# The second half of an attention layer cut into pairs, its routing moved with it, and the experts' weights loaded into tiles that an earlier layer has left

## The chip, the cores and the metric

The kernel runs on one core of one Trainium2 chip, as one program with one launch. The metric is the device time of that program in microseconds (us), the median of several executions. One further execution, the profiled one, left the trace from which all durations below come.

## The reference: what is computed

The input is x, 8 sequences of 128 tokens with 128 features, a context of 8 x 77 tokens with 128 features, and a mask. Eight blocks follow each other, each added to x: an attention over the context (L0_xattn, 16 heads of 8), a soft mixture over slots with a two-matrix feed-forward (L0_ffn), a second attention over the context (L1_xattn, 16 heads of 64), a routed mixture of 64 experts (L1_ffn), and then four larger blocks (L2_xattn, six local-attention layers, L3_xattn, two local-attention layers). All arithmetic is float32. The change touches the second attention and the routed experts. Cut to what matters, these compute:

```python
# L1_xattn, for each sequence b, 16 heads of 64
q = layernorm(x) @ w_q; k, v = split(context @ w_kv)
x = x + tanh(gate) * (softmax(q * 64**-0.5 @ k.T) @ v) @ w_out + b_out ...
# L1_ffn, over all 1024 tokens
logits = layernorm(x) @ gate_w + gate_b            # 64 experts
top3 values and experts; gates = softmax over the three
place of a token in its expert = number of earlier tokens that chose it; kept if place < 64
y[e] = gelu(rows[e] @ w1[e] + b1[e]) @ w2[e] + b2[e]   # 64 rows for each of 64 experts
x = x + sum over the kept choices of gate * y
```

The place of a token needs the choices of all tokens before it, and an expert's rows need the choices of all tokens, so the experts can start only when the last sequence has been routed.

## The kernel before, in words

**How the order is made.** The kernel is not written in execution order. Functions add steps to a plan (`Plan.add`): which engine, an estimated cost, what is read and written, which tiles are opened. `Plan.arranged` then walks through a model of time and gives each free engine the ready step of the lowest rank (the order in which steps were added), if there is room for the tiles it opens. The result is a fixed order of instructions on each engine, written into the program. TensorE (PE) gets small filler matmuls (L733) wherever this model leaves it without work in the first part, to keep its clock up. Each engine, and the queue of the sync engine SP that issues the transfers, runs its own list strictly in order.

**Tiles.** Working tiles come from pools by size: 49 tiles called `big` (512 columns), 3 `huge` (1232 columns), small ones, and 8 PSUM banks `mm`. Two large tiles, `wide` (3072 columns) and `narrow`, hold the weights of L0 (`wide`) and the padded values of its attention (`narrow`), and later the keys and values of L2_xattn. They hold nothing between the end of L0 and the fourth eighth of the experts.

**L1_xattn** (`plan_xattn_64`) works on halves of four sequences: normalize, transpose, then for each group of 8 heads the keys of all four (one matmul of 4 x 77 columns for each 128 features), the queries of all four (512 columns), and then sequence by sequence scores, softmax, values, output projection. `finish` (L1081) adds a sequence's result to x. A sequence is done after its second group.

**Routing** (`Routed.some`) takes a run of sequences: normalize (DVE statistics, POOL for the inverse root, L798 to L815, and ACT or DVE for the scaling), transpose, logits (L1310, L1311), the three best on DVE (L1320, L1322), their places (L1340 to L1358), row numbers (L1368 to L1372), and then three indirect transfers for each sequence, issued by POOL (L1387), that put the normalized rows into `expert_rows` in DRAM. It is called for sequences 0 to 3, for 4 and 5, for 6, and for 7. In the plan 4 and 5 come when the second group of sequence 5 is added.

**Experts** (`Routed.experts`, `Routed.four`): eight reads (L1445) bring `expert_rows` back, transposes turn them into `slots`. Then for each pair of experts two matmuls up (L1485), a copy, four transposes, a bias (L1495), a gelu (L1498), and eight matmuls down (L1506). Every expert needs two weight transfers of 256 KB (L1469), 128 in all, each into a `big` tile. They stand on SP's queue: 37 of them before the eight reads, 91 behind. `SPARE = 12` is the number of `big` tiles that such a prefetch must leave free in the plan; `EARLY = 4` experts are asked for at the start.

**Gates** (`Routed.gates`): the gates' normalization (L1406 to L1409), a spread of them over the experts (L1418, L1420), two more small matmul steps (transposes and L1429) and an addition to x (L1432). The plan adds them in the middle of the experts, but lets them be taken up to 600 steps ahead.

Of the kernel before, what the change touches and what calls it, by code (L numbers as in the profile page):

```python
# [24 lines left out]
P = 128  # L25
# [511 lines left out]
class Plan:  # L537
# [14 lines left out]
    def __init__(self, tc, rooms):  # L552
        self.tc, self.rooms, self.steps, self.also = tc, {k: list(range(n)) for k, n in rooms.items()}, [], []
        self.left = {k: int(self.LEFT * n + 0.9) for k, n in rooms.items()}
        self.last = {k: n // 3 for k, n in self.left.items()}
        self.latest, self.previous = {}, None
        self.warm, self.until = None, 0.0

    def fixed(self, tile):
# [48 lines left out]
    def arranged(self):  # L608
        rooms, free = self.rooms, dict.fromkeys(self.TAIL, 0.0)
# [13 lines left out]
        first = 0  # L623
        left, extra, done_on_pe = sum("PE" in s.ns for s in self.steps), 0, True

        def open_to(s):
            need = Counter(v.tag for v in s.opens)
            ahead = s.rank - first
            leaves = {k: 0 if ahead < self.NEXT // 2 else self.last[k] if ahead < self.NEAR else n for k, n in self.left.items()}
            return all(len(rooms[k]) >= n + (s.spare if s.spare and ahead else leaves[k]) for k, n in need.items())  # L630

        while times:
            t = heapq.heappop(times)
            while back and back[0][0] <= t:
                _, _, tag, slot = heapq.heappop(back)
                rooms[tag].append(slot)
            while coming and coming[0][0] <= t:
                s = heapq.heappop(coming)[2]
                for e in s.ns:
                    heapq.heappush(came[e], (s.rank, s))  # L640
            for e in free:
                if free[e] > t:
                    continue
                kept, pick, held = [], None, set()
                while came[e]:
                    rank, s = heapq.heappop(came[e])
# [10 lines left out]
                if pick is None:  # L657
                    if e == "PE" and t < self.until and t >= free[e] + (self.IDLE if done_on_pe else 0.0) and (
                            rooms["mm"] and left and (coming or any(free[x] > t for x in free if x != e))):
                        s = Step(first, {e: self.WARM}, self.warm(rooms["mm"][-1]), None, None, 0, None)  # L660
# [14 lines left out]
                s = pick  # L675
# [320 lines left out]


BUFS_A = {"tiny": 30, "few": 3, "row": 6, "big": 49, "huge": 3, "w": 1, "wr": 1}
EARLY = 4
SPARE = 12  # L1000


def plan_front(w, early, dram, wide, narrow):

    c, nc, plan, a = w.c, w.c.nc, w.plan, w.c.a
    c.room("w1", early)

    places = Context.places(plan, wide, narrow)
    lo, vals = 0, {}
    for name in ("wa", "wb", "w0"):  # L1010
        n = a[name].shape[1]
        c.packs[name], vals[name] = wide[:, lo : lo + n], plan.part(places[0], lambda t: t)
        lo += n
    come = {}

    def load(name, ns, emit, vals=None):
        come[name] = plan.fixed(None)
        plan.add({"SP": ns}, emit, [], [come[name], *(vals or [])])

    def pack(name, ns):  # L1020
        load(name, ns, lambda e: c.load(name))


    masks = [w.tile([P, 4, KC] if w.general else [KC, 4, P], I32) for _ in range(2)]
    sent = [0, 0]

    def soon(kb, emit, writes):
        sent[0] += 470
        sent[1] += kb
        plan.add({"SP": 470}, emit, [], writes, tail=max(2000.0, 2000.0 + 3.3 * sent[1] - sent[0]))  # L1030

    def x_in(b0, n):
        soon(64 * n, lambda e: nc.sync.dma_start(c.x[:, b0 : b0 + n, :], a["x"][b0 : b0 + n].rearrange("b s d -> s b d")),
              w.xs[b0 : b0 + n])

    def context(h):
        come["ctxT", h] = plan.fixed(None)
        at = slice(4 * h * KC, 4 * (h + 1) * KC)
        soon(154, lambda e: nc.sync.dma_start(c.ctxT[:, at], a["ctxT"][:, at]), [come["ctxT", h]])

    def mask(h):
        at = slice(4 * h, 4 * h + 4)
        soon(154, lambda e: nc.sync.dma_start(
            masks[h](), a["mask"][at].rearrange("b s k -> s b k") if w.general else a["maskT"][:, at, :]), [masks[h]])

    x_in(0, 2)
    soon(131, lambda e: c.load("wa"), [vals["wa"]])
    context(0)
    if w.general:
        mask(0)  # L1050
    soon(256, lambda e: c.load("wb"), [vals["wb"]])
    x_in(2, 2)
    context(1)
    x_in(4, 4)
    if w.general:
        mask(1)
    pack("col", 600)
    plan.add({"SP": 2500}, lambda e: c.load("w0"), [], [vals["w0"]])
    pack("row", 3800)
    pack("w1", 6500)  # L1060
    pack("cst", 3000)
    pack("wg", 200)
    if not w.general:
        mask(0)
        mask(1)
    route = Routed(w, early, dram, come)
    pack("w", 3000)
    pack("w3kv", 1700)
    for e in range(EARLY):
        route.weights(e)  # L1070

    tg = w.once.tile([P, 1], F32, name="tg")
    tgv = plan.fixed(tg)

    def gate(e):
        nc.scalar.activation(tg, c.get("row", "L1_xattn_gate"), AF.Tanh)
        nc.scalar.preload_act_table_set("natural_log_exp_and_others")

    def finish(b, out):
        x = w.xs[b]  # L1080
        plan.add({"DVE": 282}, lambda e: nc.vector.scalar_tensor_tensor(x(), out(), tg, x(), ALU.mult, ALU.add),  # L1081
                 [x, out, tgv], [x])

    l0x, vzs = plan_l0_xattn(w, masks, places[1], come, vals["wa"], vals["wb"])
    parts = ((0, 2), (2, 2), (4, 4))
    for part in parts:
        l0x(*part)
        plan.also = []
    plan.add({"ACT": 3000}, gate, [come["row"]], [tgv])
    if not w.general:  # L1090
        plan.add({"DVE": 2500}, lambda e: small_scores(c, (("L2_ffn", 6), ("L3_ffn", 2))), [come["row"]], [])
        for h in range(2):
            zero = w.tile([KC, 4, P])
            plan.add({"DVE": 600}, lambda e, h=h, zero=zero: nc.vector.tensor_scalar(
                zero(), masks[h](), 0.0, 2.0 * SUM_MOST, ALU.is_equal, ALU.mult), [masks[h]], [zero])
            plan.add({"DVE": 683}, lambda e, h=h, zero=zero: nc.vector.tensor_reduce(
                c.masked[:KC, h : h + 1], zero().rearrange("k b s -> k (b s)"), AX.X, ALU.max), [zero], [])
    plan.also = [vals["w0"], come["col"]]
    l0f = plan_l0_ffn(w)
    for part in parts:  # L1100
        l0f(*part)
    plan.also = [come["w1"], come["row"], come["col"]]
    l1x = plan_xattn_64(w, 8, c.get("w1", "L1_q"), c.get("w1", "L1_kv"),
                        c.get("w1", "L1_o").rearrange("p (c d) -> p c d", d=P), c.get("col", "L1_xattn_ln_gamma"),
                        c.get("col", "L1_xattn_ln_beta"), c.get("row", "L1_xattn_b_out"), finish)
    for _ in l1x(0):
        pass

    then = {3: (0, 4), 7: (4, 2), 8: (6, 1), 9: (7, 1)}
    for i, _ in enumerate(chain(l1x(1), [None]), 1):  # L1110
        if i in then:
            plan.also, also = [come["cst"], come["row"], come["wg"]], plan.also
            route.some(*then[i])
            plan.also = also
    plan.also = [come["col"]]
    route.experts(Context(w, places, vals.values(), vzs))
    plan.also = []
    return route

# [151 lines left out]
class Routed:  # L1271
# [24 lines left out]
    def some(self, b0, n):  # L1296

        w = self.w
        c, nc, plan = w.c, w.c.nc, w.plan
        at, xs = slice(b0, b0 + n), w.xs[b0 : b0 + n]  # L1300
        xh = w.tile([P, n, P])
        w.normed(lambda k: xh()[:, k, :], lambda k: xs[k](), xs, [xh], n=n)
        xT = w.tile([P, n, P])
        tp = w.turn(lambda k: xh()[:, k, :], [xh], opens=[xT], n=n)
        w.copy(xT, tp, [tp], [xT], 591, 682)
        lp, lg = w.bank([P, n, NE]), w.tile([P, n, NE])

        def logits(e):
# [7 lines left out]
        topv, efv, gatev = plan.fixed(top), plan.fixed(ef), plan.fixed(gate)  # L1316
# [14 lines left out]
        hot, chosen, before = w.tile([P, TOPK, n, NE]), self.chosen[:, at], self.before[:, at]  # L1331
# [22 lines left out]
        t, pos = w.tile([P, TOPK, n, NE]), self.pos[:, at]  # L1354
# [7 lines left out]
        validv, srcv, dstv = plan.fixed(valid), plan.fixed(srci), plan.fixed(dsti)  # L1362
# [35 lines left out]
    def gates(self, b0, n, hot, gatev, validv):  # L1398
# [9 lines left out]
            nc.vector.tensor_tensor(gate, gate, spread(gs, TOPK, 2), ALU.mult)  # L1408
            nc.vector.tensor_tensor(gate, gate, valid, ALU.mult)  # L1409

        plan.add({"DVE": 683}, weigh, [gatev, validv], [gatev])

        by_e, t2, by_eT = w.tile([P, n, NE]), w.tile([P, n, NE]), w.tile([NE, n, P])

# [4 lines left out]
                if k:  # L1419
                    nc.vector.tensor_tensor(by_e(), by_e(), t2(), ALU.add)  # L1420

        plan.add({"DVE": 5 * (200 + 75 * n)}, spread_gates, [hot, gatev], [by_e, t2])
        tp = w.turn(lambda k: by_e()[:, k, :], [by_e], NE, opens=[by_eT], n=n)
        w.copy(by_eT, tp, [tp], [by_eT], 591, 682)
        out = w.bank([P, n, P])
# [38 lines left out]
    def weights(self, e):  # L1464

        if e not in self.fetched:
            self.fetched[e] = pair = [self.w.tile([P, 4, P]) for _ in range(2)]
            for i, wt in enumerate(pair):
                self.w.plan.add({"SP": 870}, lambda _, wt=wt, i=i: self.w.c.nc.sync.dma_start(  # L1469
                    wt().rearrange("p c n -> p (c n)"), self.w.c.a["experts"][e, i]), [], [wt], spare=SPARE)  # L1470
        return self.fetched[e]

    def four(self, q, u, part, b1):

# [203 lines left out]
def plan_xattn_64(w, nch, wq, wkv, wo, gamma, beta, bias, finish, kept=None):  # L1678
# [61 lines left out]
            if j < n - 1:  # L1740
                yield

    return (part, ahead, kept) if kept else half 


class Kept:
# [660 lines left out]
```

## Time and profile before

| | |
|---|---|
| time of the runs | 1454.45 us median of 3 (1451.59 to 1457.88) |
| the profiled execution | 1436.21 us |
| its span (first to last instruction) | 1434.4 us |
| mean granted TensorE clock | 0.985 |
| busy, of the span | PE 93%, DVE 77%, ACT 59%, POOL 59% |
| last addition to x by L1_xattn | 250.48 us after the start of the span |
| first experts' matmul (L1485) | 280.40 us |
| last experts' matmul (L1506) | 373.2 us |
| first layer of local attention (L1919) | from 446.6 us |

All times inside the execution count from the start of the span. A "busy" PE includes the filler matmuls, so its share alone does not say how much of the time is needed. A float32 matmul leaves two records in the trace, a transpose one. "Idle before, releaser" is the time an engine stood still ahead of a group and what ended that; in a wait for the SP queue the releaser is what freed the tile or delivered the data.

### The profile page before, as it was taken

To read this page: it belongs to the slowest core of one execution; us is meant where nothing else is said; L and a number is where in the kernel's file an instruction comes from. 1 tells how busy PE (TensorE), PEld (TensorE's weight loads), DVE (VectorE), ACT (ScalarE), POOL (GpSimd) and SP (SyncE) were. 2 spreads that over 40 slices of the span, in tenths; PEclk is the share of its full clock that TensorE was granted. 3 is DMA by queue.
4 is the path that set the end of the run, shared out by engine and by line. 5 is a ranking of instruction groups with operands and counts; after the bars stand their busy time and mean duration, and the time that the engine had idled before them with its cause. 6 is when DMAs were issued, how large, how long until landed. Compare 5 with 4: busy or idle time off the path is not lost. (4 is left out here: it accounts for less than half of the span.)

```text
span 1434.4 us, 39795 instructions
## 1 busy us (share of the span) xinstructions
PE 1338.0 (93%) x15481; PEld 950.8 (66%) x15481; DVE 1109.2 (77%) x2350; ACT 850.7 (59%) x1775; POOL 842.3 (59%) x1367
## 2 busy tenths in 40 slices
PE   9999999898989899999999999999999999999996
PEld 7777767665576557567666676666666667665664
DVE  7543676433368898998999999999899996888882
ACT  5666565253435457567656676656667667666663
POOL 5210136401467887787687777777777772658661
PEclk9999999999989899999999999999999999999998
DMA  9401001389340357456445644754454553224330
GB/s 319 166 1 45 2 2 48 119 281 370 115 141 2 118 184 238 138 171 201 153 140 177 217 136 135 251 167 152 157 191 144 169 172 104 88 69 156 125 115 21
DMA packets 218781, 204.42 MB, mean 143 GB/s; under 512 B 31790, under 2 KB 167534, under 8 KB 217432
## 3 DMA queue, kind: packets, MB, share of 16 engines
q1 hardware_dynamic: 212696, 196.54, 42.0%
q0 software_dynamic: 1536, 3.15, 0.7%
q8 instruction: 124, 2.03, 0.6%
q10 hardware_dynamic: 4352, 2.10, 0.5%
q14 instruction: 73, 0.60, 0.1%
HBM read 129.49 MB, written 70.68 MB: 140 GB/s over the span
## 5 line engine op out<-in xcount | busy, mean ns | idle before, releaser
L1946 POOL TENSOR_TENSOR big<-big,big 128x512 f32<-128x512 f32 x224 | 284.6, 1278 | 110.8 <-DVE big L1943 87.8
L1919 PE MATMUL mm<-wide,big 128*128 128x512 f32 x672 | 310.8, 601 | 2.3 <-DVE y_res L2007 1.2
L771 ACT COPY big<-mm 128x512 f32<-128x512 f32 (+6 forms) x298 | 150.9, 517 | 157.0 <-PE mm L784 45.9
L1959 POOL TENSOR_TENSOR big<-big,few 128x512 f32<-128x512 f32 x224 | 227.4, 1043 | 1.9
L1798 DVE STREAM_TRANSPOSE big<-big 128x512 f32<-128x512 f32 (+1 forms) x248 | 209.9, 867 | 15.0 <-POOL big L1959 12.0
L1940 ACT ACTIVATE big<-mm 128x512 f32<-128x512 f32 x224 | 132.3, 596 | 144.9 <-PE mm L1919 139.8
L1919 PEld LDWEIGHTS mm<-wide,big 128*128 128x128 f32 x672 | 120.9, 191 | 124.3 <-issue 107.3
L1941 DVE TENSOR_TENSOR big<-mm,big 128x512 f32<-128x512 f32 x224 | 153.8, 687 | 13.8 <-ACT big L1940 11.5
L1943 DVE TENSOR_TENSOR big<-mm,big 128x512 f32<-128x512 f32 x224 | 153.3, 684 | 0.8 <-ACT big L1940 0.7
L1945 DVE TENSOR_REDUCE few<-big 128x8 f32<-128x512 f32 x224 | 151.5, 676 | 0.7 <-ACT big L1940 0.7
L2035 ACT ACTIVATE big<-mm 128x512 f32<-128x512 f32 x224 | 120.6, 600 | 35.0 <-PE mm L2028 32.3
L2003 PEld LDWEIGHTS mm<-narrow,big 128*128 128x128 f32 x896 | 108.9, 194 | 41.8 <-DVE big L2057 20.9
L2003 PE MATMUL mm<-narrow,big 128*128 128x128 f32 x896 | 116.8, 282 | 18.8 <-DVE big L2057 11.1
L2028 PEld LDWEIGHTS mm<-big,big 64*64 64x64 f32 x3584 | 124.9, 207 | 2.6 <-issue 1.9
L2028 PE MATMUL mm<-big,big 64*64 64x64 f32 (+2 forms) x3584 | 125.4, 274 | 1.2 <-DMA big<-blocks 1.1
L2095 PEld LDWEIGHTS mm<-big,big 128*32 128x32 f32 x3072 | 87.0, 110 | 28.9 <-issue 27.4
L2095 PE MATMUL mm<-big,big 128*32 128x128 f32 x3072 | 94.1, 273 | 0.5 <-issue 0.5
L784 PE MATMUL mm<-ident,big 128*128 128x128 f32 (+1 forms) x486 | 71.6, 282 | 24.2 <-DVE big L773 5.2
L784 PEld LDWEIGHTS mm<-ident,big 128*128 128x128 f32 (+1 forms) x486 | 54.7, 144 | 48.2 <-DVE big L773 10.5
L773 DVE COPY big<-mm 77x512 f32<-77x512 f32 (+5 forms) x89 | 52.5, 603 | 31.2 <-PE mm L1253 12.0
L2057 DVE SCALAR_TENSOR_TENSOR big<-mm,big 128x512 f32<-128x512 f32 x112 | 73.5, 684 | 1.9
L1495 DVE TENSOR_TENSOR big<-mm,p_col 128x512 f32<-128x512 f32 x32 | 20.7, 686 | 67.5 <-PE mm L784 57.5
(288 smaller groups left out, 2523.9 us busy)
## 6 DMA issues: line engine op xcount, KB each, us to landing
blocks<-big SPq DMA_DIRECT2D x224, 256.0 KB, 2.1
big<-blocks SPq DMA_DIRECT2D x224, 256.0 KB, 3.3
big<-in_experts_dram SPq DMA_DIRECT2D x128, 256.0 KB, 4.8
wide<-in_l2a_dram SPq DMA_DIRECT2D x6, 1536.0 KB, 8.9
narrow<-in_l2b_dram SPq DMA_DIRECT2D x6, 534.0 KB, 5.9
narrow<-in_l2o_dram SPq DMA_DIRECT2D x6, 512.0 KB, 6.3
blocks<-big SPq DMA_DIRECT2D x24, 128.0 KB, 1.7
big<-blocks SPq DMA_DIRECT2D x24, 128.0 KB, 3.1
```

What stands on the lines that cost most here:

```text
L771: nc.scalar.copy(out(), in_())
L1798: plan.add({"DVE": 150 + 138 * n}, lambda e: nc.vector.transpose(*within(u(), t())), [t], [u])
L1919: self.plan.add({"PE": 892}, lambda e: nc.tensor.matmul(ps(), lhsT=hs()[:, j, :], rhs=wqkv()[:, o : o + 512], start=True, stop=True), [hs, ...
L1940: yield lambda e: nc.scalar.activation(sq(), heads(), AF.Square)
L1941: yield lambda e: nc.vector.tensor_tensor(t1(), heads(), spread(rot()[:, 2 * kind, :], 8, 1), ALU.mult)
L1943: yield lambda e: nc.vector.tensor_tensor(halves(t2()), halves(heads())[:, :, ::-1, :], sin(), ALU.mult)
L1945: yield lambda e: nc.vector.tensor_reduce(ss()[:, lo : lo + 8], sq(), AX.X, ALU.add)
L1946: yield lambda e: nc.gpsimd.tensor_tensor(t1(), t1(), t2(), ALU.add)
L1959: plan.add({"POOL": 1062}, lambda e, t=t, t1=t1, i=i: nc.gpsimd.tensor_tensor(t().rearrange("p (c g d) -> p g c d", c=4, g=8), t1().rearra ...
L2003: nc.tensor.matmul(out(), lhsT=oT()[:, k, :], rhs=wo()[:, 4 * g + k, :], start=(g == 0 and k == 0), stop=(4 * g + k == nch - 1))
L2028: nc.tensor.matmul(sc[s]()[at : at + 64, k, q:end], lhsT=kT()[lo : lo + 64, k, at : at + 64], rhs=of_q(k, lo, q, end), start=False, stop=( ...
L2095: nc.tensor.matmul(avs[half]()[32 * t : 32 * t + 32, k, :], lhsT=vs[t // 2]()[:, at : at + 32], rhs=prs[t]()[:, k, :], start=True, stop=True)
```

## The change

Five edits in the first part of the program; everything from L2_xattn on stays as it is.

1. The second half of L1_xattn is normalized and transposed for its four sequences at once as before, but then runs in pairs: both groups of heads for sequences 4 and 5, then both for 6 and 7. Its keys come in matmuls of 2 x 77 columns and its queries in matmuls of 256 columns. The calls of the routing stay at steps 3, 7, 8 and 9 of it, so that sequences 4 and 5 are complete earlier than before. Routing of one or two sequences scales on DVE, and POOL's part of the normalization is two instructions instead of four.
2. The weights of experts 2 to 4 are loaded into `wide`, of 5 and 6 into `narrow`, of 7 into one `huge` tile (`weights_in`), once L0 has left them. Only experts 0 and 1 are asked for at the start.
3. The rule for the other prefetches asks for 14 free `big` tiles up to a point near the end of L1_xattn (`plan.calm`) and for 6 behind it. The plan's cost of one such transfer is 740 instead of 870.
4. The first two steps of the gates may be taken only 40 steps ahead of the oldest open step (`within=LATE`).
5. The keys and values of L2_xattn must wait for the experts whose weights lie in `wide` and `narrow`.

```diff
+            spare = s.spare and s.spare[self.calm is not None and first >= self.calm]
+            return all(len(rooms[k]) >= n + (spare if spare and ahead else leaves[k]) for k, n in need.items())
...
-EARLY = 4
-SPARE = 12
+SPARE, SPARE_LATER = 14, 6
+LATE = 40
...
-    for e in range(EARLY):
-        route.weights(e)
+    route.weights(0)
+    route.weights(1)
...
+    def idle(wide_was, narrow_was):
+
+        own = {0: [*wide_was], 1: [*narrow_was]}
+        for e, (k, lo) in enumerate(((0, 0), (0, 1024), (0, 2048), (1, 0), (1, 1024)), 2):
+            own[k] += route.weights_in(e, (places[k], lambda t, lo=lo: t[:, lo : lo + 1024]), own[k][: len((wide_was, narrow_was)[k])])
+        for e in range(7, 8):
+            route.weights_in(e, (w.tile([P, 1232]), lambda t: t))
+        return own[0], own[1]
...
+    plan.also = []
+    was = idle(vals.values(), vzs)
...
-    for _ in l1x(0):
+    for _ in l1x(0, 4):
...
-    for i, _ in enumerate(chain(l1x(1), [None]), 1):
+    for i, _ in enumerate(chain(l1x(4, 4, (0, 2), (2, 2)), [None]), 1):
+        if i == 8:
+            plan.calm = len(plan.steps)
...
-    route.experts(Context(w, places, vals.values(), vzs))
+    route.experts(Context(w, places, *was))
...
-        w.normed(lambda k: xh()[:, k, :], lambda k: xs[k](), xs, [xh], n=n)
+        w.normed(lambda k: xh()[:, k, :], lambda k: xs[k](), xs, [xh], n=n, on_dve=n < 4)
...
-        plan.add({"DVE": 683}, weigh, [gatev, validv], [gatev])
+        plan.add({"DVE": 683}, weigh, [gatev, validv], [gatev], within=LATE)
...
-        plan.add({"DVE": 5 * (200 + 75 * n)}, spread_gates, [hot, gatev], [by_e, t2])
+        plan.add({"DVE": 5 * (200 + 75 * n)}, spread_gates, [hot, gatev], [by_e, t2], within=LATE)
...
-                self.w.plan.add({"SP": 870}, lambda _, wt=wt, i=i: self.w.c.nc.sync.dma_start(
-                    wt().rearrange("p c n -> p (c n)"), self.w.c.a["experts"][e, i]), [], [wt], spare=SPARE)
+                self.w.plan.add({"SP": 740}, lambda _, wt=wt, i=i: self.w.c.nc.sync.dma_start(
+                    wt().rearrange("p c n -> p (c n)"), self.w.c.a["experts"][e, i]), [], [wt], spare=(SPARE, SPARE_LATER))
...
+    def weights_in(self, e, place, was=()):
+
+        plan = self.w.plan
+        whole, *rest = place
+        self.fetched[e] = pair = [plan.part(whole, lambda t, i=i: rest[0](t)[:, 512 * i : 512 * i + 512].rearrange(
+            "p (c n) -> p c n", n=P)) for i in range(2)]
+        for i, wt in enumerate(pair):
+            plan.add({"SP": 470}, lambda _, wt=wt, i=i: self.w.c.nc.sync.dma_start(
+                wt().rearrange("p c n -> p (c n)"), self.w.c.a["experts"][e, i]), [], [wt, *was])
+        return pair
```

In the order of instructions that the changed plan gives, SP issues 49 of the 128 weight transfers before the eight reads and 79 behind them. The order on every engine is the same as before from the first layer behind the experts on.

More of the change, by code (lines that the diff above doesn't have):

```diff
@@ L556, in __init__ @@
         self.latest, self.previous = {}, None
+        self.calm = None
         self.warm, self.until = None, 0.0
@@ L629, in open_to @@
             leaves = {k: 0 if ahead < self.NEXT // 2 else self.last[k] if ahead < self.NEAR else n for k, n in self.left.items()}
-            return all(len(rooms[k]) >= n + (s.spare if s.spare and ahead else leaves[k]) for k, n in need.items())
+            spare = s.spare and s.spare[self.calm is not None and first >= self.calm]
+            return all(len(rooms[k]) >= n + (spare if spare and ahead else leaves[k]) for k, n in need.items())
         while times:
@@ L1301, in some @@
         xh = w.tile([P, n, P])
-        w.normed(lambda k: xh()[:, k, :], lambda k: xs[k](), xs, [xh], n=n)
+        w.normed(lambda k: xh()[:, k, :], lambda k: xs[k](), xs, [xh], n=n, on_dve=n < 4)
         xT = w.tile([P, n, P])
         tp = w.turn(lambda k: xh()[:, k, :], [xh], opens=[xT], n=n)
-        w.copy(xT, tp, [tp], [xT], 591, 682)
+        w.copy(xT, tp, [tp], [xT], 180 + 103 * n, 145 + 134 * n)
         lp, lg = w.bank([P, n, NE]), w.tile([P, n, NE])
@@ L1741, in group @@
                 yield
-    return (part, ahead, kept) if kept else half
+    return (part, ahead, kept) if kept else half if nch == 4 else part
 class Kept:
```

## The prediction

> **What bounds the kernel now.** I read the page first: PE is busy for 93% of the span, so a gain must come from a place where PE waits or does filler work. Then I cut the front part into stages and read the busy time of each engine in each stretch (columns: stretch, its length, busy time and count of PE, weight loads, DVE, ACT, POOL, then clock, DMA share, GB/s).
>
> ```profile
> 150.00:252.00 102.00, 97.83 (x1181) 72.36 (x1179) 71.05 (x215) 61.91 (x193) 42.17 (x73) 1.00 0.07 21
> 252.00:275.00 23.00, 21.48 (x168) 19.35 (x167) 17.13 (x92) 3.45 (x11) 14.59 (x30) 1.00 0.13 43
> 275.00:281.00 6.00, 2.53 (x10) 1.68 (x12) 0.00 (x0) 1.08 (x2) 0.00 (x0) 0.80 0.66 190
> 281.00:320.00 39.00, 35.77 (x347) 24.80 (x344) 9.30 (x16) 23.54 (x45) 0.00 (x0) 0.99 0.89 287
> 320.00:373.00 53.00, 44.96 (x455) 28.74 (x453) 20.55 (x34) 18.49 (x36) 6.88 (x9) 1.00 0.83 296
> ```
>
> The first row is L1_xattn: PE waits for only 4.2 of 102 us. The second and third are the gap between it and the experts, where PE's 21.48 us are mostly filler. The last two are the experts: PE waits for 3.2 and 8.0 us, and the DMA engines are near full.
>
> What sets the gap's end is POOL's and SP's timeline (columns: start, duration, instruction, idle before and what ended it):
>
> ```profile
> 254.04 0.21 POOL L815 TENSOR_TENSOR tiny<-tiny,tiny 128x1 f32<-128x1 f32 x1
> 259.20 1.09 POOL L1387 DMA_INDIRECT expert_rows<-big,dsti  x1 [4.96 <-issue]
> ...
> 272.08 0.96 POOL L1387 DMA_INDIRECT expert_rows<-row,dsti  x1 [0.22 <-issue]
> ...
> 273.35 0.95 POOL L1387 DMA_INDIRECT expert_rows<-row,dsti  x1 [0.22 <-issue]
> ```
>
> Twelve transfers for sequences 4 to 7 run back to back from 259.20 to 274.30, 1.26 us each. POOL sets the end; DVE has the numbers of sequence 7 ready at 267.43, six us before its last transfer. SP and PE then follow:
>
> ```profile
> 29.17 221.60 SPq L1469 DMA_DIRECT2D big<-in_experts_dram  x37
> 275.72 5.19 SPq L1445 DMA_DIRECT2D big<-expert_rows  x8
> 282.27 15.34 SPq L1469 DMA_DIRECT2D big<-in_experts_dram  x19
> ```
> ```profile
> 303.57 55.00 SPq L1469 DMA_DIRECT2D big<-in_experts_dram  x72
> ```
> ```profile
> 248.32 2.05 PE L992 MATMUL mm<-p_w,big 128*128 128x128 f32 x16
> ...
> 271.96 2.50 PE L733 MATMUL mm<-ident,ones 128*128 128x128 f32 x18
> 278.47 2.00 PE L784 MATMUL mm<-ident,big 128*128 128x128 f32 x8 [4.00 <-DMA big<-expert_rows]
> 280.40 6.13 PE L1485 MATMUL mm<-big,slots 128*64 128x512 f32 x24
> ...
> 292.19 5.46 PE L1506 MATMUL mm<-big,big 128*64 128x128 f32 x96 [0.26 <-ACT big L1498]
> ...
> 364.05 0.66 PE L784 MATMUL mm<-ident,big 128*128 128x128 f32 x4 [0.88 <-DVE big L773]
> ```
>
> Call T the end of the last projection, 250.37. From T to the first transpose of returned rows PE spends 28.1 us (278.47); the rows come 4.2 us behind the last put (274.30). From there to the last matmul down (373.18) are 94.7 us. Everything behind has the same order on all engines in both programs, so I let it shift as a block: a us saved here is a us at the end.
>
> **The change, part by part.**
>
> *Before T.* The same columns go through PE; keys of 154 and queries of 256 columns only split them. ACT pays 383 ns for a scaled tile of 256 columns against 597 for 512, so each of 8 split queries costs 2 x 383 - 597 = 169 ns; a copied key tile of 308 columns takes 416, one of 154 about 290 by the slope to the 256-column copy (370), so 164. Sixteen splits: 2.7 us over ACT (61.9 busy of 102) and DVE (71.1 of 102), beneath PE's 97.8. If ACT or DVE were what PE waits for, it would all count. Out of this stretch go four value matmuls of L2_xattn (0.31 us each, -1.2) and the spread of the first gates on DVE (L1418, L1420, about 2.0). In L0 the new program holds 8 fillers fewer ahead of T, 34 for 42, where 11 of them (22 records) took 2.62 us: -1.9. That is a count of places without work, so its worth lies between -3 and 0. I take -2 for everything ahead of T, between -4 and +5.
>
> *The gap.* In the new order sequences 4 and 5 are routed ahead of the last projections. Their numbers are ready about 2.4 us ahead of T: DVE still has the statistics of sequence 6, two aggregates and three operations of L2's keys (0.29 + 0.17 + 2 x 0.53 + 0.48 + 0.3) before the last addition to x. The trace puts 1.1 us between ready numbers (258.1) and the put (259.20), so POOL starts at T - 1.1. Its list is then: one put (1.26), root of 6 (L798, L812 only: 0.19 + 0.58, about 0.85 with the waits), three puts, root of 7, two puts, then 6's and 7's. The root of 7 is queued behind four puts and ends at -1.1 + 1.26 + 0.85 + 3.8 + 0.85 = T + 5.6. From there the chain of one sequence, by the pieces of the trace: scaling and transpose 0.8, copy 0.4, logits 0.6, copy and three best 1.3, comparison 0.5, choice 0.75, places on PE 0.75, then 0.75 and 0.85 on DVE, 1.1 to the put: 7.8; DVE also finishes sequence 6 in between, +0.6. Puts of 7 from T + 14.0 to T + 17.8; rows at T + 22.0 against 28.1: **-6.1**. Best case, no queueing behind those four puts, -9; worst case, sequences 4 and 5 late by 4 us, -2. PE's 57 fillers and small work need about 19 us and lie under this. The gates' DVE work (about 8 us in 258 to 272) is no longer among the steps of 7; that is in the chain above.
>
> *The experts.* PE is busy for 83.46 of the 94.8 us from 278.4 on. L2's keys leave for the gap (-2.2); its values (+1.2) and the gates' transposes and biases (1.5 + 2.6) come in: 86.6. Waits: 11.3 now. At the start the new order transposes returned rows behind the first two matmuls up, where 24 matmul records stood before, and SP's seventh read reuses a tile of the second: some 2 us of wait. In the last third the order before runs one group of four experts at a time and loses 0.88 us in each; the new order takes eight or more experts at once, as long as weights are there. I count 5 us of wait in all: 91.6, **-3.1**.
>
> Are weights there? Twelve more transfers have arrived by then, 3.1 MB, or 12 x 0.764 = 9.2 us of the steady row (55.00/72 = 0.764 us each). The other 79 need 79 x 0.764 = 60.4 us. The Trainium skill (DMA: Bandwidth & Descriptors, Where 436 GB/s comes from) gives a core about 358 GB/s from HBM, 0.73 us each, so 57.8; the page's rule (Bandwidth, Measured) to make transfers of 1 MiB or more, since each pays a fixed 2.0 us (Anatomy of one DMA), would give 79 x 2.6 = 205 us and speaks against loading by 256 KB. The trace decides for the row: up to 392 GB/s between 350 and 360 us, the fixed part hidden because many are in flight. But the rooms of experts 2 to 7 are used once, so their use frees no tile: I count 4 or 5 transfers in the first 13 us behind the first matmul up, where 19 came in 15.3 us before. From then on 75 x 0.764 = 57, landing 4.8, and the 10 us by which the last matmul trailed the last landing: 13 + 57 + 5 + 10 = 85 us, from a start 1.9 us behind the transposes: 87. That is just inside PE's 91.6, with nothing to spare. Bounds: -6 (hardly a wait) to +3. If this cover is gone, the excess counts in full, since the gathers of L2_xattn wait for the last expert.
>
> *Hidden.* The zeroing and keys in `narrow` and `wide` wait for experts 2 to 6 and come behind all puts on POOL, which is idle from 281 to 320; L2's values stand behind 40 experts' matmuls. If they were late, PE would wait for them inside the experts. The gates' 9 us of DVE lie in a stage where DVE is busy for 29.9 of 94.8. The prefetches ahead of the reads wait for tiles freed around T and land by T + 8, ahead of the reads at T + 19.
>
> Sum: -2 - 6.1 - 3.1 = **-11.2 us**. Against its own execution that is 1436.2 - 11.2 = 1425.0. The runs' median lies 18.2 above the profiled one; I keep the difference: 1454.45 - 11.2 = **1443.2**.
>
> **The rivals.**
>
> *Full cover* (chance 0.16): weights are always there and L0 gives its 3 us: -3 - 8 - 6 = -17, 1437. For it: DMA moved 392 GB/s when asked. Against: the first 13 us free so few tiles.
>
> *Pairs cost what the gap gains* (0.18): with two sequences in flight instead of four PE waits for softmax. DVE already waits 12.3 us for the scores (L834 behind L970), and PE only has the other pair's work to fill in. The 2.7 us of splits and some 3 us of bubbles turn -2 into +4: total -5, 1449, within what a measurement can tell.
>
> *Starved experts* (0.16, the slower side): transfers behind the reads stay bound by tiles. Between 282 and 320 the program before issued 19 in 15.3 us, then none for 6 us, about 1.08 us each over 38 us. If all 75 ran so, 13 + 81 + 15 + 1.9 = 111 us in place of 94.7, and with -8.1 from the other parts the total is +8: 1462. It is slower than before from about 0.97 us for a transfer on.
>
> **How the numbers follow.** The forecast itself has 0.50; its own range is -7.5 to -15, 1439 to 1447. About 0.5% (7.3 us) is what a measurement of this kernel tells from no change. Faster: 0.50 + 0.16 = 0.66; same 0.18; slower 0.16. The range reaches from the full cover to the first part of the starved case: 1435 to 1459.
>
> **What would show it.** First transpose of returned rows 21 to 23 us behind the last projection, POOL's puts of 4 and 5 beginning ahead of T; 49 transfers issued ahead of the reads; the experts taking about 91 us with fewer 0.88 us waits; no stretch of SP waiting for PE beyond the first 13 us. Wrong would be: T later than 252; the experts' matmuls up waiting for weights; or the stages behind the experts growing by what the front saves.

## The result, and the profile after

The changed kernel takes 1432.6 us (median of 4, 1428.1 to 1434.9) beside 1453.5 for the kernel before: ratio 0.985, 95% interval 0.981 to 0.989, so 20.9 us less where 11.2 were forecast. The time lies 2.4 us below the predicted range. Its profiled execution took 1430.38 us (span 1428.5, clock 0.984) and, unlike that of the kernel before, lies among its timed runs. From one profiled execution to the other the gain is only 5.8 us. Most of the runs below are about this puzzle, 20.9 against 5.8.

The same stages of the changed kernel, with T (the end of the last projection) now at 257.8, not at 250.4 (columns: stretch, its length, busy time and count of PE, weight loads, DVE, ACT, POOL, then clock, DMA share, GB/s):

```profile
150.00:250.00 100.00, 94.65 (x1138) 73.62 (x1138) 65.03 (x206) 58.03 (x191) 37.65 (x61) 0.97 0.07 20
258.00:280.20 22.20, 16.97 (x137) 15.48 (x135) 9.20 (x46) 0.94 (x4) 12.64 (x23) 1.00 0.25 82
280.20:320.00 39.80, 38.62 (x365) 26.50 (x366) 17.58 (x54) 23.26 (x42) 7.20 (x7) 1.00 0.73 232
320.00:367.50 47.50, 46.13 (x469) 31.43 (x467) 16.20 (x34) 23.75 (x45) 0.00 (x0) 1.00 0.89 318
```

L1_xattn got slower: T comes 7.4 later, and from 150 us to T PE is busy for 102.5 of 107.8 us, where it was busy for 96.2 of 100.4 before. The gap fell from 28.1 to 22.4, and in the experts PE waits 2.6 us of 87.3 instead of 11.3 of 94.7. POOL's list in the gap (timeline; L1402 is the former L1387):

```profile
256.23 1.01 POOL L1402 DMA_INDIRECT expert_rows<-big,dsti  x1 [3.99 <-DVE tiny L807]
...
262.36 0.57 POOL L814 TENSOR_TENSOR tiny<-tiny,mhalf 128x1 f32<-128x1 f32 x1
...
272.25 0.96 POOL L1402 DMA_INDIRECT expert_rows<-row,dsti  x1 [2.81 <-DVE valid L1391]
...
274.78 0.96 POOL L1402 DMA_INDIRECT expert_rows<-row,dsti  x1 [0.21 <-issue]
```

The first put (indirect transfer) of sequence 4 starts 1.6 us ahead of T, and POOL's share of the root of sequence 7 ends at T + 5.1, as forecast (1.1 and 5.6). But the first put of sequence 7 waits 2.8 us for DVE, which itself stood still. Two lines of DVE's timeline show a kind of wait that the profile of before does not have anywhere:

```profile
242.66 0.48 DVE L836 TENSOR_REDUCE tiny<-mm 128x4 f32<-128x308 f32 x1 [5.63 <-remote]
...
270.35 0.35 DVE L1372 TENSOR_TENSOR big<-big,mm 128x192 f32<-128x192 f32 x1 [3.10 <-remote]
```

"Remote" means that no instruction of another engine accounts for the release. I call such a wait of 2 us or more a stall. POOL's 2.8 us come from the second one. SP's queue:

```profile
246.29 10.26 SPq L1484 DMA_DIRECT2D big<-in_experts_dram  x8
277.15 5.91 SPq L1460 DMA_DIRECT2D big<-expert_rows  x8
283.58 72.50 SPq L1484 DMA_DIRECT2D big<-in_experts_dram  x79
```

The 79 transfers take 72.5 us, 0.92 each. Their one line hides a pause of 9.2 us between the first (283.58) and the next (292.76). It is the longest wait of SP's queue for a tile (from 255 to 375 us; who waited for whom, us in total, times, longest):

```profile
SPq L1484 <- PE mm L786: 10.6, 7, 8.8
```

Before, the longest pause in this stretch was 6 us (297.6 to 303.57). PE hardly felt it: all its waits for weights in the changed experts come to 1.2 us.

### The profile page after: what moved, and what is told of

It reads as the page before. It is cut to its first block, busy times and chain, and to the rows that moved or that the text cites. A ratio compares the mean times of both kernels' runs of the same rounds, so it can differ in the third digit from the quotient of the medians.

```text
span 1428.5 us, 39805 instructions
## 1 busy us (share of the span) xinstructions
PE 1340.3 (94%) x15487; PEld 955.7 (67%) x15487; DVE 1107.3 (78%) x2362; ACT 851.2 (60%) x1779; POOL 842.4 (59%) x1357
## 3 DMA queue, kind: packets, MB, share of 16 engines
q8 instruction: 124, 2.03, 0.6%
## 5 line engine op out<-in xcount | busy, mean ns | idle before, releaser
L773 ACT COPY big<-mm 128x512 f32<-128x512 f32 (+7 forms) x311 | 157.0, 519 | 161.1 <-PE mm L786 40.7
L1824 DVE STREAM_TRANSPOSE big<-big 128x512 f32<-128x512 f32 (+1 forms) x248 | 210.0, 866 | 16.4 <-POOL big L1985 14.7
L786 PE MATMUL mm<-ident,big 128*128 128x128 f32 (+1 forms) x486 | 69.4, 279 | 11.3 <-DMA big<-expert_rows 3.5
L855 POOL TENSOR_TENSOR big<-big,tiny 128x308 f32<-128x308 f32 x38 | 27.2, 722 | 84.1 <-DVE tiny L852 30.7
L775 DVE COPY big<-mm 128x512 f32<-128x512 f32 (+6 forms) x84 | 45.8, 558 | 27.1 <-PE mm L1268 12.0
```

What stands on the lines that cost most here:

```text
L773: nc.scalar.copy(out(), in_())
L1824: plan.add({"DVE": 150 + 138 * n}, lambda e: nc.vector.transpose(*within(u(), t())), [t], [u])
```

## The experiments

The kernel before was timed beside every group of runs. Its median was 1450 to 1454 us in four of the six groups, the first comparison's 1453.5 among them, and 1435.4 and 1435.7 in the two others. A single profiled execution need not be of its group's kind: the first one took 1436.2, and the runs of the first comparison 1451.6 to 1457.9. Some expectations speak of "a chip with stalls"; that it is the chip is not shown, and one chip number is on record for a group of each kind. All ratios are to the kernel before of the same group, without which the numbers below could not be read.

### The kernel before, again

No edit.

> The kernel before, unchanged, profiled and timed anew: its timed runs lay 17 us above its profiled execution (1453.5 against 1436.2), those of the changed kernel did not (1432.6 against 1430.4). If the first profile was a lucky draw: a new profiled execution near 1453, with some 17 us of idle time that the first does not show (the places: waits on nothing visible, or a lower granted clock), timed runs near 1453. If profiling itself takes those us off this kernel: again a profiled execution near 1436 and timed runs near 1453. If the timed runs had some passing disturbance: both near 1436.

Median 1451.3 (20 runs), ratio 0.9992 (0.998 to 1.0005), profiled at 1452.7. So the first profile, at 1436.2, was not typical of the timed runs that I set it against. The list of waits between 220 and 300 us shows the difference (columns: who waited for whom; us in total, times, longest):

```profile
DVE tiny L834 <- remote: 10.8, 1, 10.8
...
DVE big L1357 <- remote: 7.3, 1, 7.3
...
PE mm L970 <- issue: 6.4, 10, 1.1
```

In it T is at 260.2 (first profile 250.4), the gap takes 33.0 (28.1), the experts 93.2 (94.7), and what lies behind 1064.5 (1061.2). PE's timeline inside the first stall and at its end:

```profile
231.17 0.33 PE L970 MATMUL mm<-big,big 64*64 64x77 f32 x3 [0.49 <-issue]
232.61 0.36 PE L970 MATMUL mm<-big,big 64*64 64x77 f32 x3 [1.10 <-issue]
233.35 0.38 PE L970 MATMUL mm<-big,big 64*64 64x77 f32 x1 [0.38 <-issue]
...
238.30 1.01 PE L970 MATMUL mm<-big,big 64*64 64x77 f32 x21 [0.42 <-issue]
```

PE gets one to three records of matmuls every 0.7 or 1.4 us, while nothing in the profile holds it back; then it takes up its pace at once. The granted clock is no rival cause: it was 1.00 in both profiles up to 233.3 us, when DVE had stood still for 5.8 us. It was 0.50 from there to 247.0, beyond the end of the stall, so the lower clock is a part of what the stall costs. From 150 us to T, PE waits 7.7 us instead of 4.2 and is busy for 102.5 instead of 96.2 with the same work. Every "remote" wait of 2 us or more in this and in the profiles of the changed kernel falls into one of the three stretches where POOL issues indirect transfers: 220 to 247, 254 to 289 and 369 to 440 us. I took them as the suspect.

### Are POOL's indirect transfers the cause?

The first twelve left out, so rows of sequences 0 to 3 stay zero (on both kernels, in the same order otherwise; the edit with a line around it):

```diff
                 def put(e, j=j, k=k):
+                    if b0 == 0:
+                        return
                     if plan.previous == "put":
```

> The kernel before with POOL's first twelve indirect transfers (inputs of the experts for sequences 0 to 3) left out, so those rows stay zero; all else in the same order. Theory 'a row of indirect transfers on POOL starves the other engines of instructions': in the repeated profile of before, TensorE runs L970 in bits of 2 to 4 matmuls between 229 and 238 us and DVE's L834 starts 10.8 us late, and both resume when the twelve are over. Without them that stall is gone, the last projection ends at about 250 instead of 260, the second stall (7.3 us, in the other twelve) stays: about 1442, -8 to -11. Theory 'engines reload instructions there anyway': the stall stays, the last projection ends at about 259, 1450 to 1453.

> The changed kernel with the same twelve indirect transfers (sequences 0 to 3) left out, those rows stay zero. Starvation theory: the 5.6 us stall of DVE and the trickle of TensorE in 235 to 243 us go, and so does the queue that the twelfth transfer makes: the last projection ends at 249 to 251 instead of 257.8, -6 to -8 against the changed kernel, so 1425 to 1427. If the stall is there anyway: 1431 to 1433.

The same twelve as plain transfers of 64 KB from SP's queue, to fixed rows (in part; the memsets between them go too):

```diff
-                    put = nc.gpsimd.indirect_dma_start(
+                    at_row = P * (3 * j + k)
+                    put = nc.sync.dma_start(self.rows[at_row : at_row + P, :], xh()[:, j, :]) if b0 == 0 else nc.gpsimd.indirect_dma_start(
```

> The kernel before with the first twelve indirect transfers of POOL replaced by plain transfers of the same 64 KB each from SP's queue to fixed rows, so rows land in other places than routed. It tells the transfers' traffic from POOL's way of issuing them. If POOL's issuing starves the engines: no stall, as without the twelve, about 1442. If any 12 x 64 KB in those 16 us hold the instruction loads: the stall stays, 1450 to 1453.

These fell into a group where the kernel before took 1435.4. Without the twelve 1433.7 (ratio 0.9988, 0.9971 to 1.0005), made plain 1433.5 (0.9981), and no stall in any profile: nothing to take away, so they could not tell. The changed kernel without the twelve took 1418.8. Repeated, they met a group with a before of 1450.9:

> The kernel before without POOL's first twelve indirect transfers (those rows stay zero), on another chip. Where the kernel before takes about 1452 beside it (a chip with stalls): if the twelve transfers starve the other engines, the stall of some 10 us in 228 to 238 us is gone, the last projection ends at 248 to 250 instead of 260, -9 to -13 against before, 1439 to 1443. If the engines reload instructions there anyway, the stall stays: within 3 us of before. Where before takes about 1435: -2, as measured there.

> The kernel before with these twelve transfers as plain ones from SP's queue to fixed rows. On a chip with stalls: if POOL's way of issuing is what starves the engines, as without the twelve, 1439 to 1443; if the traffic itself does, within 3 us of before. On a chip without: -2.

Without the twelve 1440.5 (0.994, 0.9915 to 0.9966), made plain 1437.6 (0.9905, 0.9873 to 0.9937), with T at 248.8 and 248.0: as the first theory had it, the second a little below its 1439. The row from 230 to 240 us, first of the repeated kernel before, then of the one with plain transfers:

```profile
230.00:240.00 10.00, 4.48 (x68) 3.05 (x69) 1.64 (x5) 1.14 (x6) 5.13 (x9) 0.67 0.12 40
```
```profile
230.00:240.00 10.00, 8.71 (x74) 6.22 (x72) 9.90 (x28) 6.51 (x29) 2.80 (x4) 1.00 0.01 3
```

DVE is busy for 9.9 instead of 1.6 us. Without indirect transfers the first stall is gone, worth 10 to 13 us; the bytes alone don't bring it back. Beside the other twelve, a stall stayed in the profile without the first twelve (its ACT waits 10.4 us there, up to 274.67), and there was none in the one with plain transfers. So a row of indirect transfers goes with a stall but does not bring one each time.

Is it their density? Eight memsets of one element ahead of each:

```diff
-                    if plan.previous == "put":
-
+                    for _ in range(8 if b0 == 0 else plan.previous == "put"):
                         nc.gpsimd.memset(self.between, 0.0)
```

> The changed kernel with eight tiny memsets on POOL ahead of each of the first twelve indirect transfers, so that these come about 2 us apart instead of 1.26. If only an unbroken row of them starves the engines: the stall of 5.6 us shrinks to 0 to 2, the last projection ends at 251 to 254, 1427 to 1430 in all. If each transfer holds the instruction loads by itself, however spaced: the stall is as long or longer (the row lasts 25 us instead of 16), and POOL's own work for the softmax (L855) comes later: 1433 to 1440.

> The changed kernel with eight tiny memsets ahead of each of the first twelve transfers, which puts these 2.2 to 2.6 us apart. On the chip without stalls it took 1428.6 with the last projection ending at 263.2, and the row of twelve ended at 254.7: POOL's softmax work (L855) waits in the row. On a chip with stalls: 1430 to 1436 if spacing takes away the stalls and costs what it cost there, over 1440 if the stalls come on top.

1428.6 beside a before of 1435.4, and 1432.2 beside 1450.9, where the changed kernel itself took 1427.9. The first says nothing of density, since its group had no stalls to take away; that it lies in the 1427 to 1430 of one theory is luck, as T came at 263 and not at 251 to 254. In the second group the profile, with most transfers 2.2 to 2.5 us apart, has no stall at that place. It is one profile, and the fastest of four runs (1425.5 to 1440.5), so that spacing keeps the stall away is likely and not shown. T came at 263 here too: POOL's divisions for the softmax (L855) stand in its list behind the spaced transfers. Spacing gained nothing.

### The change where there are stalls and where there are none

No edit; the changed kernel in three groups.

> The changed kernel anew. The kernel before has a typical time of 1452 on one chip, with three stalls beside POOL's indirect transfers (10.8, 7.3 and 3.0 us), and of 1435 on another, with none. By the traces the changed kernel, without its own stalls (5.6 and 3.1 us), would be 17 us below a before without stalls. Theory 'the change saves its own 17 wherever it runs': beside a before of 1435 it takes 1416 to 1420, beside one of 1452 it takes 1430 to 1435. Theory 'most of the 21 us were stalls that it met less of': beside 1435 it takes 1424 to 1430.

> The changed kernel. On a chip with stalls: 1430 to 1433 beside 1450 to 1453, as twice before. On a chip without: if the change saves 17 by itself, 1416 to 1420 beside 1435; if most of the 21 us were stalls, 1424 to 1430.

> The changed kernel once more, on the chip of a_plan8. Beside a before of about 1451: 1428 to 1432. Beside a before of about 1435 (no stalls): 1416 to 1420 if the change saves 17 by itself, 1424 to 1430 if most of the 21 us were stalls that it meets less of.

1430.5 beside 1450.2 (0.9864, 0.9823 to 0.9905), 1427.9 beside 1450.9 (0.9832, 0.9789 to 0.9875), and 1419.8 beside 1435.7 (0.9895, 0.9871 to 0.9919). Where the kernel before has no stalls (one group) the change saves 15.9 us and takes 1419.8, inside the first theory's 1416 to 1420. Where it has them it saves 20 to 23. The third profile has no "remote" wait at all; its stages (the gap, and the experts in three pieces):

```profile
250.50:270.70 20.20, 16.91 (x138) 15.55 (x136) 9.50 (x46) 0.94 (x4) 12.83 (x23) 1.00 0.27 91
270.70:280.00 9.30, 9.30 (x50) 5.36 (x52) 1.38 (x2) 6.53 (x11) 1.36 (x2) 0.82 0.73 200
280.00:320.00 40.00, 40.00 (x420) 28.97 (x417) 20.18 (x62) 20.52 (x40) 5.83 (x5) 1.00 0.80 273
320.00:359.30 39.30, 37.01 (x368) 24.73 (x364) 12.30 (x22) 19.60 (x36) 0.00 (x0) 1.00 0.84 296
```

| us (one profile each, but the last) | before, no stalls | changed, no stalls | before, stalls | changed, stalls (mean of 3 profiles) |
|---|---|---|---|---|
| T | 250.4 | 250.5 | 260.2 | 257.2 |
| T to first transposes of rows | 28.1 | 20.2 | 33.0 | 21.2 |
| from there to last matmul down | 94.7 | 88.6 | 93.2 | 87.8 |
| the rest of the span | 1061.2 | 1056.8 | 1064.5 | 1062.7 |

The rest is scatter: over the seven profiles without any stall it runs from 1057 to 1063 us, for either kernel and its variants. The difference of the two columns on the left is 0 - 7.9 - 6.1, on the right -3.0 - 11.8 - 5.4. So the stalls add 3 us at T and 4 in the gap to what the change brings by itself. In three of four profiles the changed kernel meets no stall in the gap.

### The parts one at a time

Onto the kernel before: the pairs alone, the weights in rooms (`wide`, `narrow`, `huge`) alone, the gates alone. The edits are shown in part; with the pairs goes what edit 1 says of the routing.

```diff
-    for _ in l1x(0):
+    for _ in l1x(0, 4):
...
-    for i, _ in enumerate(chain(l1x(1), [None]), 1):
+    for i, _ in enumerate(chain(l1x(4, 4, (0, 2), (2, 2)), [None]), 1):
```
```diff
-EARLY = 4
+EARLY = 2
...
+    was = idle(vals.values(), vzs)
...
+    route.experts(Context(w, places, *was))
```
```diff
+        plan.add({"DVE": 683}, weigh, [gatev, validv], [gatev], within=LATE)
+        plan.add({"DVE": 5 * (200 + 75 * n)}, spread_gates, [hot, gatev], [by_e, t2], within=LATE)
```

> Only the pairs: the second half of L1_xattn and the inputs of routed pairs, the rest as before. My steps: the gap shrinks by about 6 us, the experts as before. The order shows 105 fillers ahead of the last projection where the kernel before has 42 (each about 0.24 us by the row of 11 fillers in 2.62 us, so up to 15 us of places without other work). Theory 'each part brings its own gain': -6, about 1447. Theory 'pairs need the tiles that the weights leave': the last projection ends some 10 to 15 us later, and the total is +4 to +9, 1457 to 1462.

> Only the weights of experts 2 to 7 in the rooms that the first layer leaves: 49 transfers ahead of the row reads instead of 37. Theory 'each part brings its own gain': the experts take 87 to 90 us instead of 94.7, the rest is as before, -5 to -7: about 1447. Theory 'the gain is in the whole': within 3 us of before. If the 17 us between timed and profiled runs of before come from the place or number of the weights' transfers ahead of the first layer's end, the timed runs fall to about 1430 with this alone.

> Only the gates moved back (40 places), the rest as before: their 8 us of DVE leave the chain of sequences 6 and 7, but POOL's twelve transfers in a row still set the end of the gap. By my steps: 0 to -2, 1451 to 1454. If the gates were what holds the numbers of the last sequence: -4 to -6.

Beside a before of 1452.6: pairs 1461.5 (1.0072, 1.0049 to 1.0096), rooms 1452.5 (1.0004, 0.9989 to 1.0019), gates 1458.1 (1.0036, 1.0006 to 1.0066). No part alone gains, and two lose. With pairs alone T comes at 274.9, the gap takes 25.4 and the experts 94.3: the gap gains, and L1_xattn loses more. This profile has no stall of 2 us ahead of 400 us, so beside the first profile of before T is 24.5 later and the span 19.3 longer; the 9 us of the timed runs are less, probably because they stand beside runs of before with stalls. Its PE is busy for 119.0 us from 150 to T, where the kernel before has 96.2 to 102.5; 63 fillers more at 0.24 are 15 of them. With rooms alone the experts take 89.5, but the profile at 1443.1 was the lowest of 20 runs, so where its other runs lose those us again stays open. With the gates alone the rows are back earlier (first read at 283.8, 290.3 in the repeated before), but 61 records of fillers stand ahead of the transposes, which begin at 293.1 (293.2), so nothing is gained; a case of the kind is shown below. Why they cost 5.5 us stays open.

Taken from the changed kernel: the same edits undone (in part), with the spares of 14 and 6 kept.

```diff
-    for _ in l1x(0, 4):
+    for _ in l1x(0):
```
```diff
-    route.weights(0)
-    route.weights(1)
+    for e in range(4):
+        route.weights(e)
...
-    was = idle(vals.values(), vzs)
```
```diff
-        plan.add({"DVE": 683}, weigh, [gatev, validv], [gatev], within=LATE)
+        plan.add({"DVE": 683}, weigh, [gatev, validv], [gatev])
```

> The changed kernel with L1_xattn's second half and the inputs of routed sequences as before (no pairs), weights in idle rooms, spares and moved gates kept. By my steps the pairs are worth the gap's 6 us (earlier start of POOL's row for sequences 4 and 5): it is then 5 to 8 us slower than the changed kernel of the same call. If pairs bring nothing by themselves: within 2 us of it. If they cost more ahead of the last projection than they save: 3 us faster or more.

> The changed kernel without the rooms: experts 0 to 3 early as before, 38 transfers ahead of the row reads instead of 49, pairs, spares and moved gates kept. The order shows 75 fillers ahead of the last projection where the changed kernel has 34, since eight tiles of L1_xattn's are held by weights. Theory 'rooms make the pairs possible': the last projection ends some 10 us later and the experts take 94 instead of 87 to 88 us: 12 to 20 us slower than the changed kernel, no better than the kernel before. Theory 'rooms are worth only the weights': 5 to 7 us slower.

> The changed kernel with the gates of routed pairs where they were (no 40 places back). They are 8 us of DVE ahead of or among the steps of sequence 7. If this order matters: POOL's last transfers come 2 to 4 us later and the time is 2 to 4 us longer than the changed kernel of the same call. If they lie beside POOL's row: within 1 us.

Beside the changed kernel's 1430.5: without pairs 1438.7 (0.993 of before, 0.9908 to 0.9953), without rooms 1449.6 (1.0003, 0.9981 to 1.0026), without the gates' delay 1432.8 (0.9873, 0.9829 to 0.9917, which the scatter covers). So pairs are worth 8 us and rooms 19 where the other is there, about the sizes expected, and nothing where it is not. Both were measured only in groups with stalls. Without rooms T is 269.8, with 41 fillers more ahead of it. Most of them stand in one block (64 records are 32 fillers), beside POOL's first row of transfers:

```profile
236.17 8.84 PE L735 MATMUL mm<-ident,ones 128*128 128x128 f32 x64
```

There the plan found no work for PE for 9 us; with the rooms it finds some. The reason that I gave for it, tiles held by weights, is not borne out: in that stretch weights hold 30 `big` tiles without rooms (24 and 6 transfers by then) and 29 with them. Why the plan comes out so stays open. The experts still take 88.0 us without the rooms, 89.5 with the rooms alone and 92 with the later gates alone, so more than one part can shorten them; the spares were not tried by themselves.

The profile without pairs shows a further cost where PE is fed in bits. PE's timeline at the end of its gap:

```profile
273.15 0.37 PE L735 MATMUL mm<-ident,ones 128*128 128x128 f32 x1 [1.03 <-issue]
273.85 0.37 PE L735 MATMUL mm<-ident,ones 128*128 128x128 f32 x1 [0.33 <-issue]
274.55 8.21 PE L735 MATMUL mm<-ident,ones 128*128 128x128 f32 x58 [0.33 <-issue]
282.61 1.04 PE L786 MATMUL mm<-ident,big 128*128 128x128 f32 x8
```

The fillers trickle from 267 us on, while POOL's last transfers run and land, and the 58 records of them that are left must be worked off before the transposes, though SP issued the first read at 273.9. Transposes come 8.7 us behind that read, 2.6 to 3.0 in the changed kernel's profiles. So a part of the 8 us that the pairs are worth can be this delay. Fillers that were written in to fill a gap are in the way when the engine loses time inside it.

### An attempt to have the rest back

Spaced transfers as above, and the planner told what they cost, so that it gives most divisions in that stretch to DVE:

```diff
-                plan.add({"POOL": 1050}, put, [dstv, xh], [self.rowsv], "put")
+                plan.add({"POOL": 1050 if b0 else 2250}, put, [dstv, xh], [self.rowsv], "put")
```

> The changed kernel with eight tiny memsets ahead of each of the first twelve indirect transfers, as in the spaced one, and their price in the planner raised from 1050 to 2250 ns, so that it gives the softmax's division (L855) to DVE while POOL's row lasts: in the order one division stands among the twelve where the changed kernel has four. Spaced alone, there was no stall but the last projection ended at 262.7. If that loss was the divisions queued behind spaced transfers: the last projection ends at 250 to 253 without a stall, 1420 to 1425 beside the changed kernel's 1428 to 1432. If DVE becomes what PE waits for instead: 256 to 262, 1428 to 1434.

1428.5 beside the changed kernel's 1419.8 and a before of 1435.7 (ratio to before 0.9952, 0.993 to 0.9974). T comes at 251.2 as hoped. But POOL's row now ends where the next should have begun:

```profile
256.35 1.06 POOL L1401 DMA_INDIRECT expert_rows<-big,dsti  x1 [0.17 <-issue]
257.42 0.09 POOL L1400 MEMSET between<- 1x1 f32 x1
257.72 0.96 POOL L1401 DMA_INDIRECT expert_rows<-big,dsti  x1 [0.21 <-issue]
```

The first put of sequence 4 starts at 257.7 instead of 248.9, the last ends 6.1 us later, and the transposes begin 6.2 later (276.8, 270.7). It missed both expectations: they rested on T and left POOL's list out. Whether it pays where there are stalls was not tried. No version that beats the changed kernel came out.

## Why the prediction was right and wrong

*The step that failed* is "The runs' median lies 18.2 above the profiled one; I keep the difference". It left the difference as something that no change could touch. It was inside: by the second profile of before 9.8 us at T, 4.9 in the gap, -1.5 in the experts and 3.3 behind, with stalls beside POOL's indirect transfers that the first profiled execution did not have. With the change some 4 to 7 us of that go, as the savings with and without stalls show (20 to 23 against 15.9); why it meets less of them is not shown. Of the 9.7 us by which the forecast of -11.2 missed, 5.0 are this; the other 4.7 are sizes: the gap 1.8 and the experts 3.0 too small, T 2 too good, and 1.9 in the rest, within its scatter. The trace of before could not show the stalls, but an offset of 18 us, 2.5 times what a measurement can tell from nothing, should have been a case of its own with a range on both sides.

*Before T, -2*: 0 in the profiles without stalls (250.4 to 250.5), -3 with them. Nothing of the 1.9 for 8 fillers fewer and the 1.2 for moved matmuls shows at T. By the slope that it names, a key tile of 154 columns takes 280 ns and not 290, which is 0.2 us in all. Between like profiles the bounds of -4 to +5 held.

*The gap, -6.1*: right in mechanism and somewhat small, -7.9 without stalls. The pieces: first put of 4 at T - 1.5, root of 7 at T + 5.1, last put over at T + 15.9 instead of 17.8, transposes at T + 20.2 instead of 22.0. The term that was too large is the chain of sequence 7 from root to first put: 7.3 us measured (255.63 to 262.96), 8.4 counted with DVE's other work. With stalls the gap gained 11.8, more than the best case of -9.

*The experts, -3.1*: too small, -6.1 without stalls, -5.4 with. PE's busy time was right, 86.3 counted as 86.6. Mis-sized is "I count 5 us of wait in all": it was 2.3, nearly all of it five waits for weights of 0.35 to 0.59 us, and the waits of 0.88 us are gone. The dry start came as counted: 6 transfers in the first 13 us behind the first matmul up (4 in the three profiles with stalls), for 4 or 5 forecast, and DMA moved 69 to 120 GB/s from 275 to 285 us, then 219 to 366 up to 310. The row of 79 took 73.2 us, and not 13 + 57. The rule of 1 MiB and 2.0 us that the prediction set aside stands on its page for transfers that GpSimd issues, while SP issues these; the 205 us are an estimate from it, and the row did not come near it.

*The rivals.* Full cover is what happened in the experts and the gap, -6 and -8, without its 3 us ahead of T. "Pairs cost what the gap gains" points the right way for the pairs alone, which cost 9 us in all; with the rooms beside them that cost is gone, and I had counted the rooms only as weights that come earlier. Starved experts: wrong. Its 1.08 us for a transfer came from a stretch that held a pause of 6 us, and it added a dry start on top. Behind the first 13 us the other 73 transfers started 0.81 us apart, below its 0.97.

*What I named as signs*: transposes at 21 to 23 us behind T held in the first profile (22.4), and they came at 20.2 to 20.8 in the others; the puts beginning ahead of T and 49 transfers held; the experts took 87 to 89 us, not about 91; matmuls up did wait for weights, but for 1.2 to 2.4 us in all; "wrong would be T later than 252" came true (257.8) and was a stall, not the pairs, as the profile without stalls has T at 250.5.

## What to carry to other kernels

Ask of an offset between a profile and the timed runs what it is made of before adding it to a forecast; a second profile of the same kernel answered that here, and a trace that shows no stall does not show that the timed runs have none. The parts of a change to a planned order don't add up: alone they brought +9, 0 and +5.5 us, together (with the spares) -21, so judge the order of the whole. The fillers counted ahead of T told its two late ends before any run did: 75 and 105, T at 270 and 275, against 34 and 42 at 250 to 260. Filler work stands in an engine's list like any other, so it covers a gap only as long as the engine gets through it.

## What the runs showed of the hardware

Beside rows of indirect transfers on POOL, 1.26 us apart for the most part, DVE and ACT stood still for 2 to 12.8 us and PE got one to six records of matmuls every 0.7 or 1.4 us, in four of six groups of runs, though not in each of their profiles, and not at all in two. Leaving the row out or making it plain took the stall away at that place; with the row spaced, the one profile that could show a stall there had none. What decides between the two kinds of group the runs don't show.

Nor do they show what is held back. That PE starves with no wait to account for it made me think of its instructions: the profile has them arrive by DMA queues of their own (q8 of 124 packets and 2.03 MB, 16.4 KB each). The Trainium skill (Runtime: NRT & Kernel Launch, Instruction fetch mechanics) has the same blocks and calls the cost of passing from one to the next mostly hidden. Over most of the 1430 us the trace agrees. Inside the first stall of the repeated kernel before, one block arrives from 229.0 to 230.2 us, near its start, and the next packet of instructions begins at 240.5. PE takes up its pace at 238.3, between the two, so it was not the arrival of a block that set it going. How the transfers bring the stalls about stays open.
